# Last queries' steps of a decoder kernel: the sine part of the rotations moved to GpSimd, tree operations and product additions interleaved differently, and one block product issued earlier

## The chip, the cores and the metric

The kernel runs on one core of a Trainium2 chip. The engines of a core have instruction queues of their own: TensorE (PE; its weight loads are listed as PEld), VectorE (DVE), ScalarE (ACT), GpSimd (POOL) and SyncE (SP, which here only issues DMAs; ACT issues some too). The metric is the device time of one execution in microseconds (us), given as the median of several runs.

## The reference

Two decoder layers over x of shape (2, 512, 1024), all in float32 at the interfaces. The change touches only the start of the second layer's attention:

```python
x = x + _L0_xattn_ref(_layernorm(x), ctx, ...)      # quantized product
x = x + _L0_ffn_ref(_layernorm(x), ...)             # linear with routed low-rank part
x = x + _L1_xattn_ref(_layernorm(x), ctx, ctx, mask, wq, wk, wv, wo, 0)
x = x + _L1_ffn_ref(_layernorm(x), ...)             # linear with gated low-rank part

# in _L1_xattn_ref: 32 query heads, 8 key/value heads, 128 wide
q = _apply_rope(q, curr_seq_pos)                    # x * cos + rotate_half(x) * sin
raw = jnp.einsum('bhqd,bhkd->bhqk', q, k) / scale
attn = jax.nn.softmax(raw + mask, axis=-1)
out = jnp.einsum('bhqk,bhkd->bhqd', attn, v)
```

Queries are 512 long, keys and values 1024 long.

## The kernel before

**Products.** The large products are done as one level of a Strassen-like scheme: seven block products (`seven`, L270, in the order 1, 2, 6, 7, 5, 4, 3) give four blocks of 128 x 512. Each block product is four matmuls of 128x128 by 128x512 into a PSUM bank (`accumulate`, L345; its matmul is L347). The results are combined by additions on VectorE (L288, L291, L293, L297, L300). A finished block of queries is handed to `emit` (L664), which starts a rotation (`rope_steps`, L213). A rotation is two half copies on ScalarE (L216, L217: the rotated half of the block), then on VectorE `dst = acc * scale * cos` (L219), `rot = rot * sin` (L222) and `dst = dst + rot` (L223), and a DMA that writes the block to DRAM (L662).

**The last queries and the attention share steps.** Queries are made in eight groups of four heads. The eighth group (heads 28 to 31 of both batches, 2 x 7 = 14 block products, called a1, b1, a2, b2, then a6 a7 a5 a4 a3, then b6 b7 b5 b4 b3 after the two halves `head(0)` and `head(1)` and the block number) isn't made at once: `attention` (L836) draws its products one by one with `next(extra["products"])`. Of each rotation only the ScalarE copies are issued with the product; the rest is put on a list `later` and issued further on in the step.

**A step of the attention** is one turn of the loop at L860, with n from -2. It works on three heads at once: `new` = head n+2, `mid` = head n+1, `old` = head n.

- Scores of `new` (L743): four times two matmuls (L748) into a two-bank PSUM tile `wide`, each followed on VectorE by the addition of the mask into SBUF (L762). There are two `wide` tiles, taken in turn, so scores 2 needs the L762 of scores 0 to be done.
- The maximum over keys, `tree` (L766): four VectorE operations L770, L772, L774 (128 x 1024, all operands in SBUF) and L776 (128 x 512).
- Block products of the last queries or, for n over 4, of the output projection (`projection`, L824, through `seven_onto`, L304).
- `turn_sum` of `old` and `turn_maximum` of `new` (L779, L783): four transposes on TensorE into a `wide` tile (L712), a reduction on VectorE (L714, for the sum also L785), and a trip through DRAM by ScalarE's DMA queue (L721, L727) that comes back spread over all partitions. A `wide` tile used here is free for scores again once L714 is done.
- `exponential` of `mid`, twice: L794 on VectorE (128 x 2048, one operand in SBUF, the maximum in PSUM, put there by ScalarE at L790), L797 on ScalarE, and the sums over keys on GpSimd (L800; then L803, L804, L805).
- `attend` of `old`, twice four matmuls (L811), each time after one of the two turns; ScalarE copies the result out (L819), GpSimd multiplies by the reciprocal sum one step later (L822).

In the loop the order on TensorE, VectorE, ScalarE and GpSimd is the order of the program; each queue runs its instructions in that order. SyncE's queue holds the loads of queries, keys, values and weights, and the writes L662. At n = 4, 8, ... GpSimd also adds up operands of the projection (L245 to L253).

The number of products drawn in step n is in L1121:

```python
extra = {-2: 3, -1: 2, 0: 2, 1: 2, 2: 2, 3: 2, 4: 1}
```

and phase two and three of a step are, before the change (L892 to L927, shortened):

```python
for _ in range(3 + k % 2):
    next(stretches, None); next(tree, None)
...
for _ in range(extra.pop(n, 0)):
    next(extra["products"]); next(tree, None)
...
for steps in (tree, *extra["later"]):
    for _ in steps: pass
```

The functions in full, with the line numbers that the profile uses:

Of the kernel before, what the change touches and what calls it, by code (L numbers as in the profile page):

```python
# [15 lines left out]
ALU = mybir.AluOpType  # L16
# [6 lines left out]
GRP = NH // NKV  # L23
# [12 lines left out]
ATT_SCALE = float(np.float32(1.0) / np.sqrt(np.float32(DH)))  # L36
# [3 lines left out]
def decoder_kernel(  # L40
# [25 lines left out]
    nc = tc.nc  # L66
# [12 lines left out]
    def u8(shape, dtype=F32):  # L79
        return new(shape, "u8", 14, dtype)  # L80

    def u4(shape, dtype=F32):
        return new(shape, "u4", 17, dtype)

    def u2(shape, dtype=F32):
        return new(shape, "u2", 10, dtype)
# [61 lines left out]
    sin_t = [const.tile([P, HALF], F32, name="sin_t"), None]  # L148
# [58 lines left out]

    def rope(dst, acc, half, scale):

        for _ in rope_steps(dst, acc, half, scale):  # L210
            pass

    def rope_steps(dst, acc, half, scale):  # L213

        rot = u2([P, HALF])
        nc.scalar.activation(rot[0:64, :], acc[64:128, :], AF.Copy, scale=scale)  # L216
        nc.scalar.activation(rot[64:128, :], acc[0:64, :], AF.Copy, scale=scale)  # L217
        yield
        nc.vector.scalar_tensor_tensor(  # L219
            dst, acc, scale, cos_t[half], ALU.mult, ALU.mult  # L220
        )
        nc.vector.tensor_tensor(rot, rot, sin_t[half], ALU.mult)  # L222
        nc.vector.tensor_tensor(dst, dst, rot, ALU.add)  # L223

# [2 lines left out]
    def left_sums(eng, *args):  # L229

        return last_of(left_steps(eng, *args))
# [38 lines left out]
    def seven(product, emit):  # L270

        banks = {}
        for i in (1, 2, 6, 7, 5, 4, 3):
            first = {2: 1, 4: 7, 3: 5}.get(i, i)
            if i == first:
                banks[i] = ps_b()
            acc = banks[first]  # L280
            product(i, acc, i == first)
            if i == 1:
                u, c22, c21 = u2([P, HALF]), None, None
                nc.scalar.copy(u, acc)
            elif i == 2:
                emit(0, 0, acc)
            elif i == 6:
                nc.vector.tensor_tensor(u, u, acc, ALU.add)  # L288
            elif i == 7:
                c22 = u2([P, HALF])  # L290
                nc.vector.tensor_tensor(c22, u, acc, ALU.add)  # L291
            elif i == 5:
                nc.vector.tensor_tensor(c22, c22, acc, ALU.add)  # L293
                emit(1, 1, c22)
            elif i == 4:
                c21 = u2([P, HALF])
                nc.vector.tensor_tensor(c21, u, acc, ALU.add)  # L297
                emit(1, 0, c21)
            else:
                nc.vector.tensor_tensor(u, u, acc, ALU.add)  # L300
                emit(0, 1, u)
            yield
# [42 lines left out]
    def accumulate(acc, pairs, start):  # L345
        for k, (lhsT, rhs) in enumerate(pairs):
            nc.tensor.matmul(  # L347
                acc,
                lhsT,
                rhs,  # L350
                start=start and k == 0,
                stop=k == len(pairs) - 1,
                skip_group_check=True,
            )
# [19 lines left out]
    def halves():  # L374
        return [u8([P, 2, D]) for _ in range(2)]
# [273 lines left out]
    def queries(q, h_ops, w, later=None):  # L649

        def head(m):
            def product(i, acc, start):
                accumulate(
                    acc,
                    [(w[i - 1][:, c, ts(m, P)], h_ops[i - 1][:, c, :]) for c in range(4)],
                    start,
                )

            def finish(i, j, src):
                dst = u2([P, HALF]) if (i, j) == (0, 0) else src  # L660
                yield from rope_steps(dst, src, 0, ATT_SCALE)
                nc.sync.dma_start(q_d[j][4 * q + 2 * i + m], dst)  # L662

            def emit(i, j, src):  # L664
                steps = finish(i, j, src)
                next(steps)
                if later is None:
                    next(steps, None)
                else:
                    later.append(steps)  # L670

            return seven(product, emit)

        return head(0), head(1)
# [49 lines left out]
    def from_row(row):  # L724

        t = u2([P, S])
        nc.scalar.dma_start(t, row.partition_broadcast(P))  # L727
        return t
# [107 lines left out]
    def attention(extra):  # L836

        total = B * NH
        heads, outs, kv = {}, {}, {}
        stretches = iter(())

        def begin(n):
            if n >= total:
                return
            gg = n // GRP
            if gg not in kv:
                b, g = gg // NKV, gg % NKV  # L850
                kT = u4([P, S2])
                nc.sync.dma_start(kT, kT_d[b][g])
                v = u4([P, NKT, DH])
                nc.sync.dma_start(v, v_d[b][g // 2][:, :, ts(g % 2, DH)])
                kv[gg] = kT, v
                outs[gg] = u8([P, GRP, S])
            heads[n] = Head(n, kv[gg], outs[gg][:, n % GRP, :])

        begin(0)
        for n in range(-2, total + GRP + 1):  # L860
            new, mid, old = heads.get(n + 2), heads.get(n + 1), heads.get(n)
            begin(n + 3)
            if new:
                for j in range(4):
                    new.scores(j)
            yield

            if n - 1 in heads:
                heads.pop(n - 1).normalize()
            if n == GRP - 1 or n == NH:  # L870
                x[n // NH] = halves()
                for t, d in zip(x[n // NH], x_d[n // NH]):
                    nc.sync.dma_start(t, d)

            if GRP <= n <= total and n % GRP == 0:
                oT = outs.pop(n // GRP - 1)
                sums = u8([P, 3, 2, 256])
                places = iter(range(3))
                o_ops = left_sums(
                    nc.gpsimd,  # L880
                    oT[:, 0:2, 0:256],
                    oT[:, 2:4, 0:256],
                    oT[:, 0:2, 256:S],
                    oT[:, 2:4, 256:S],
                    lambda: sums[:, next(places)],
                )
                following = n // GRP - 1, o_ops
            tree = new.tree() if new else iter(())
            k = (n - 1) % GRP
            if n > GRP and k == 0:  # L890
                gg, o_ops = following
                stretches = projection(gg // NKV, o_ops, dict(w_ops))  # L892
            for _ in range(3 + k % 2):
                next(stretches, None)
                next(tree, None)
            if n > GRP and gg + 1 < B * NKV:
                for i in {2: (1, 6, 2), 3: (7, 5, 4, 3)}.get(k, ()):
                    w_ops[i] = output_operand((gg + 1) % NKV, i)
            for _ in range(extra.pop(n, 0)):
                next(extra["products"])  # L900
                next(tree, None)
            if n == GRP:
                w_ops = {i: output_operand(0, i) for i in (1, 6, 2, 7, 5, 4, 3)}
            for steps in (tree, *extra["later"]):
                for _ in steps:
                    pass
            extra["later"].clear()
            yield

            if mid:  # L910
                mid.place_maximum()
            if old:
                old.turn_sum()
                old.attend(0)
            if mid:
                mid.exponential(0)
            if old:
                old.den = from_row(old.den)
            if new:
                new.turn_maximum()  # L920
            if mid:
                mid.exponential(1)
            if new:
                new.nmx = from_row(new.nmx)
            if old:
                old.attend(1)
            yield  # L927
# [106 lines left out]
    for b in range(B):  # L1034
# [4 lines left out]
        for i, stage in enumerate((keys, keys, values, values)):  # L1039
# [7 lines left out]
            if i == 1 and b == 1:  # L1047
# [7 lines left out]
                hs, steps = normed(0, u8, 2)  # L1055
# [19 lines left out]
    for b in range(B):  # L1075
        main = linear(b, token_sums(hs, eights()), w_ops, lambda: tT[b], bl_t)
        if b == 0:
            hs, steps = normed(1, u8, 2)
# [24 lines left out]
    later = []  # L1103
# [14 lines left out]

    extra = {-2: 3, -1: 2, 0: 2, 1: 2, 2: 2, 3: 2, 4: 1}  # L1121
    steps = attention({**extra, "products": main, "later": later})
    stats = all_moments(0)
    last = {"zT": [None] * B, "w": [None] * 7, "h": [None] * 7}
# [42 lines left out]
    for i in range(2):  # L1167
        n = 44 + 4 * i
# [16 lines left out]
    with tc.manual_schedule(  # L1185
# [6 lines left out]
        for i in range(3 * (B * NH + 2)):  # L1192
            next(steps)
            n, phase = divmod(i, 3)
# [121 lines left out]
```

## Time and profile before

| | |
|---|---|
| median of 3 runs | 2494.17 us (2492.08 to 2495.93) |
| the profiled execution's own time | 2491.89 us |
| its span, first to last instruction | 2490.1 us |
| mean granted TensorE clock | 0.992 |
| VectorE busy | 1852.5 us (74%) |
| ScalarE busy | 527.9 us (21%) |
| GpSimd busy | 1011.8 us (41%) |
| the steps n = -2 to 4, and n = 5 up to the end of its projection products | about 937 to 1108 us of the span |
| rotations of the eighth group, VectorE part (L219, L222, L223) | first at 957.70, last at 1091.09 us |

Times in views of the trace are microseconds from the start of the span, and "us" columns are durations. A bracket like `[3.32 <-DVE small L714]` says how long the engine was idle before the instruction, and which instruction's end released it. "x8" counts instructions; each float32 matmul shows as two records, so a block product is 8 records, the scores of a head 16. In rows by stretch of time, each engine has its busy time and count, and PEclk is the TensorE clock that was granted, 1.00 being full speed.

### The profile page before, as it was taken

To read this page: it belongs to the slowest core of one execution; us is meant where nothing else is said; L and a number is where in the kernel's file an instruction comes from. 1 tells how busy PE (TensorE), PEld (TensorE's weight loads), DVE (VectorE), ACT (ScalarE), POOL (GpSimd) and SP (SyncE) were. 2 spreads that over 40 slices of the span, in tenths; PEclk is the share of its full clock that TensorE was granted. 3 is DMA by queue.
4 is the path that set the end of the run, shared out by engine and by line. 5 is a ranking of instruction groups with operands and counts; after the bars stand their busy time and mean duration, and the time that the engine had idled before them with its cause. 6 is when DMAs were issued, how large, how long until landed. Compare 5 with 4: busy or idle time off the path is not lost.

```text
span 2490.1 us, 19684 instructions
## 1 busy us (share of the span) xinstructions
PE 2434.2 (98%) x6848; PEld 1214.5 (49%) x6856; DVE 1852.5 (74%) x2036; ACT 527.9 (21%) x615; POOL 1011.8 (41%) x536
## 2 busy tenths in 40 slices
PE   7999999999999998989999999999999999999999
PEld 3477458654444443434444444444444444445454
DVE  5848774345886557988888888888898888887552
ACT  1201221011222222232222222222222222222100
POOL 0000010111000001557676767676777676667421
PEclk8999999999999999999999999999999999999999
DMA  7225233012895221343323322442334233323301
GB/s 264 103 92 204 75 124 106 26 68 106 283 329 199 76 93 47 102 131 107 84 80 109 109 83 80 138 150 79 114 106 130 62 104 114 104 74 110 127 26 43
DMA packets 148243, 283.83 MB, mean 114 GB/s; under 512 B 29296, under 2 KB 47232, under 8 KB 146352
## 3 DMA queue, kind: packets, MB, share of 16 engines
q1 hardware_dynamic: 107888, 242.25, 28.7%
q10 hardware_dynamic: 39824, 39.60, 6.6%
q8 instruction: 55, 0.90, 0.2%
q0 software_dynamic: 432, 0.71, 0.1%
q14 instruction: 44, 0.36, 0.0%
HBM read 221.44 MB, written 61.08 MB: 113 GB/s over the span
## 4 chain that ended last, share of the span: by engine, by line
PE 59%; DVE 7%; POOL 2%; issue 2%; DMA 1%; ACT 1%; SPq 0%; POOLq 0%; DVEq 0%; ACTq 0%
PE b L347 26%; PE wide L748 15%; PE b L811 15%; PE wide L712 2%; DVE u L794 2%; DMA u<-in_wo_dram 1%; PE wide L937 1%; DVE u L772 1%; DVE u L774 1%; DVE small L714 1%; POOL u L804 1%; POOL u L803 0%; DVE u L762 0%; DVE u L222 0%; DVE u L219 0%
## 5 line engine op out<-in xcount | busy, mean ns | idle before, releaser
L347 PE MATMUL b<-u,u 128*128 128x512 f32 (+1 forms) x3648 | 1408.6, 543 | 25.3 <-DVE u L291 10.8
L347 PEld LDWEIGHTS b<-u,u 128*128 128x128 f32 x3648 | 691.4, 191 | 707.5 <-issue 619.4
L748 PE MATMUL wide<-u,u 128*128 128x512 f32 x1024 | 456.9, 597 | 15.7 <-DVE small L714 8.5
L811 PE MATMUL b<-u,u 128*128 128x512 f32 x1024 | 461.2, 593 | 0.0
L800 POOL TENSOR_TENSOR u<-u 128x1024 f32<-128x1024 f32 x64 | 151.6, 2369 | 747.4 <-DMA row<-small 385.0
L762 DVE TENSOR_TENSOR u<-wide,u 128x1024 f32<-128x1024 f32 x256 | 312.7, 1224 | 128.2 <-PE wide L748 127.8
L797 ACT ACTIVATE u<-u 128x2048 f32<-128x2048 f32 x128 | 244.6, 1911 | 675.7 <-DVE u L794 626.4
L748 PEld LDWEIGHTS wide<-u,u 128*128 128x128 f32 x1024 | 193.4, 191 | 268.0 <-issue 176.8
L794 DVE TENSOR_TENSOR u<-u,b 128x2048 f32<-128x2048 f32 x128 | 290.0, 2266 | 0.0
L811 PEld LDWEIGHTS b<-u,u 128*128 128x128 f32 x1024 | 186.7, 192 | 185.2 <-issue 185.2
L322 POOL TENSOR_TENSOR u<-u,u 128x512 f32<-128x512 f32 x120 | 189.4, 1599 | 195.0 <-DVE u L320 175.4
L320 DVE TENSOR_TENSOR u<-u,b 128x512 f32<-128x512 f32 x200 | 135.7, 679 | 135.1 <-PE b L347 135.1
L803 POOL TENSOR_TENSOR u<-u,u 128x1024 f32<-128x1024 f32 x64 | 150.8, 2356 | 35.6 <-ACT u L797 34.6
L804 POOL TENSOR_TENSOR u<-u,u 128x1024 f32<-128x1024 f32 x64 | 151.9, 2374 | 5.0
L822 POOL TENSOR_TENSOR u<-u,u 128x512 f32<-128x512 f32 x64 | 119.9, 1873 | 21.4 <-DMA u<-row 21.4
L1053 POOL DMA_DIRECT2D u<-in_b_dram x1 | 0.6, 558 | 301.8 <-PE wide L450 301.8
L216 ACT ACTIVATE u<-u 64x512 f32<-64x512 f32 x72 | 45.2, 628 | 344.6 <-DVE u L293 167.3
L712 PEld LDWEIGHTS wide<-ident,u 128*128 128x128 f32 x512 | 80.2, 204 | 64.6 <-issue 54.7
L770 DVE TENSOR_TENSOR u<-u 128x1024 f32<-128x1024 f32 x64 | 111.4, 1741 | 0.0
L772 DVE TENSOR_TENSOR u<-u,u 128x1024 f32<-128x1024 f32 x64 | 106.3, 1660 | 0.2
L805 POOL TENSOR_TENSOR u<-u 128x512 f32<-128x512 f32 x64 | 102.0, 1594 | 5.0
L774 DVE TENSOR_TENSOR u<-u,u 128x1024 f32<-128x1024 f32 x64 | 97.4, 1522 | 0.2
(125 smaller groups left out, 1552.3 us busy)
## 6 DMA issues: line engine op xcount, KB each, us to landing
u<-row ACTq DMA_DIRECT2D x128, 256.0 KB, 3.7
u<-wo SPq DMA_DIRECT2D x64, 512.0 KB, 4.0
u<-in_wo_dram SPq DMA_DIRECT2D x48, 512.0 KB, 4.5
u<-in_wq_dram SPq DMA_DIRECT2D x32, 512.0 KB, 4.0
q<-u SPq DMA_DIRECT2D x64, 256.0 KB, 2.1
u<-in_wo_dram SPq DMA_DIRECT2D x16, 1024.0 KB, 8.1
wo<-u SPq DMA_DIRECT2D x32, 512.0 KB, 3.7
u<-q SPq DMA_DIRECT2D x64, 256.0 KB, 4.1
```

Of the source, the lines that this page charges most:

```text
L320: nc.vector.tensor_tensor(c, c, acc, ALU.add)
L322: nc.gpsimd.tensor_tensor(c, c, u, ALU.add)
L347: nc.tensor.matmul(acc, lhsT, rhs, start=start and k == 0, stop=k == len(pairs) - 1, skip_group_check=True,)
L748: nc.tensor.matmul(sc[:, ts(n, HALF)], self.kT[:, ts(2 * j + n, P)], self.qT, start=True, stop=True,)
L762: nc.vector.tensor_tensor(self.e[j // 2][:, js, :], sc.rearrange("p (k q) -> p k q", k=2), mask[j], ALU.add)
L772: nc.vector.tensor_tensor(m, m, e[1][:, 0:2, :], ALU.max)
L794: nc.vector.tensor_tensor(e, e, self.nmf.unsqueeze(1).to_broadcast([P, 4, S]), ALU.add)
L797: nc.scalar.activation(e, e, AF.Exp)
L800: nc.gpsimd.tensor_tensor(d, e[:, 0:2, :], e[:, 2:4, :], ALU.add)
L803: nc.gpsimd.tensor_tensor(d, d, e[:, 0:2, :], ALU.add)
L804: nc.gpsimd.tensor_tensor(d, d, e[:, 2:4, :], ALU.add)
L811: nc.tensor.matmul(self.acc, self.v[:, k, :], self.e[j][:, k % 4, :], start=(k == 0), stop=(k == NKT - 1),)
```

## The change

The rotation takes its engine as an argument. For the eighth group of queries L222 and L223 (the multiplication by the sine and the last addition) are issued on GpSimd; L219 and the ScalarE copies stay, and all other rotations stay as they were. In steps with n of 4 and less, the operations of the maximum's tree are no longer issued ahead of the loop over products: before each product two of them are issued, and what is left after the last product. The pending rotations are issued by `rotate()`, after `turn_sum` of the old head (or, where there is no old head yet, after `turn_maximum` of the new one, which thereby comes ahead of the exponentials in steps -2 and -1) instead of right behind the tree. In the table of products, step -1 draws three instead of two and step 3 one instead of two: the order of the products stays, and the sixth, eighth, tenth and twelfth are each issued one step sooner.

```diff
-    def rope_steps(dst, acc, half, scale):
+    def rope_steps(dst, acc, half, scale, eng):
...
-        nc.vector.tensor_tensor(rot, rot, sin_t[half], ALU.mult)
-        nc.vector.tensor_tensor(dst, dst, rot, ALU.add)
+        eng.tensor_tensor(rot, rot, sin_t[half], ALU.mult)
+        eng.tensor_tensor(dst, dst, rot, ALU.add)
...
-                yield from rope_steps(dst, src, 0, ATT_SCALE)
+                eng = nc.vector if later is None else nc.gpsimd
+                yield from rope_steps(dst, src, 0, ATT_SCALE, eng)
                 nc.sync.dma_start(q_d[j][4 * q + 2 * i + m], dst)
...
+        def rotate():
+            for rotation in extra["later"]:
+                next(rotation, None)
+            extra["later"].clear()
...
-            for _ in range(3 + k % 2):
+            for _ in range(3 + k % 2 if n > GRP else 0):
                 next(stretches, None)
                 next(tree, None)
...
             for _ in range(extra.pop(n, 0)):
+                for _ in range(2):
+                    next(tree, None)
                 next(extra["products"])
-                next(tree, None)
...
-            for steps in (tree, *extra["later"]):
-                for _ in steps:
-                    pass
-            extra["later"].clear()
+            for _ in tree:
+                pass
             yield
 
             if mid:
                 mid.place_maximum()
             if old:
                 old.turn_sum()
+            elif new:
+                new.turn_maximum()
+            rotate()
+            if old:
                 old.attend(0)
             if mid:
                 mid.exponential(0)
             if old:
                 old.den = from_row(old.den)
-            if new:
-                new.turn_maximum()
+                if new:
+                    new.turn_maximum()
             if mid:
                 mid.exponential(1)
...
-    extra = {-2: 3, -1: 2, 0: 2, 1: 2, 2: 2, 3: 2, 4: 1}
+    extra = {-2: 3, -1: 3, 0: 2, 1: 2, 2: 2, 3: 1, 4: 1}
```

More of the change, by code (lines that the diff above doesn't have):

```diff
@@ L208, in rope @@
     def rope(dst, acc, half, scale):
-        for _ in rope_steps(dst, acc, half, scale):
+        for _ in rope_steps(dst, acc, half, scale, nc.vector):
             pass
-    def rope_steps(dst, acc, half, scale):
+    def rope_steps(dst, acc, half, scale, eng):
         rot = u2([P, HALF])
```

## The prediction

> **What bounds the kernel now.** I read the page first, then stretches of time around the steps that change, then what TensorE waited for there, then the timelines of TensorE, VectorE and GpSimd. The page:
>
> ```profile
> PE 2434.2 (98%) x6848; PEld 1214.5 (49%) x6856; DVE 1852.5 (74%) x2036; ACT 527.9 (21%) x615; POOL 1011.8 (41%) x536
> ```
>
> TensorE sets the end; only its lost time can be won. From 1107.4 us on, the listing of TensorE shows no more gaps in the following steps, so a gain before that should last to the end. Three of the nine stretches of the early steps (busy time and count of each engine, then granted clock):
>
> ```profile
> core 0: us, PE busy (x) PEld busy (x) DVE busy (x) ACT busy (x) POOL busy (x), PEclk, DMA share, GB/s
> ...
> 972.49:993.14 20.65, 17.33 (x38) 7.47 (x37) 17.72 (x16) 3.82 (x2) 8.34 (x4) 0.83 0.12 38
> ...
> 1039.04:1060.59 21.55, 21.55 (x58) 10.06 (x57) 18.78 (x17) 4.30 (x3) 10.56 (x5) 1.00 0.33 91
> ...
> 1081.56:1107.43 25.87, 20.99 (x52) 9.10 (x53) 22.45 (x19) 7.32 (x8) 18.78 (x10) 1.00 0.46 137
> ```
>
> The turns of step 2 and the scores and products of step 3 (middle row) are pure TensorE. The turns of step 4 and the scores and products of step 5 (last row) lose some 5 us with VectorE 87% busy, and the scores of step 0 (first row) lose 3.3 us and run at a granted clock of 0.83. What TensorE waited for between 935 and 1100 us (total, times, longest):
>
> ```profile
> PE wide L748 <- DVE small L714: 8.5, 5, 3.3
> ...
> PE wide L748 <- DVE u L762: 5.7, 4, 1.6
> ...
> PE wide L712 <- POOL u L805: 1.1, 1, 1.1
> ...
> PE wide L712 <- DVE u L776: 0.9, 1, 0.9
> ```
>
> So scores wait for a `wide` tile, because VectorE comes late to L714 and L762. The largest case, first on TensorE, then on VectorE:
>
> ```profile
> 972.49 0.63 PE L712 MATMUL wide<-ident,u 128*128 128x128 f32 x4
> 972.96 1.88 PE L748 MATMUL wide<-u,u 128*128 128x512 f32 x4
> 978.16 8.28 PE L748 MATMUL wide<-u,u 128*128 128x512 f32 x12 [3.32 <-DVE small L714]
> ```
>
> ```profile
> 972.69 0.69 DVE L288 TENSOR_TENSOR u<-u,b 128x512 f32<-128x512 f32 x1 [1.26 <-PE b L347]
> 973.30 0.68 DVE L219 SCALAR_TENSOR_TENSOR u<-b,cos_t 128x512 f32<-128x512 f32 x1
> 973.90 0.68 DVE L222 TENSOR_TENSOR u<-u,sin_t 128x512 f32<-128x512 f32 x1
> 974.61 0.69 DVE L223 TENSOR_TENSOR u<-u,u 128x512 f32<-128x512 f32 x1
> 975.22 2.28 DVE L794 TENSOR_TENSOR u<-u,b 128x2048 f32<-128x2048 f32 x1
> 977.42 0.68 DVE L714 TENSOR_REDUCE small<-wide 128x4 f32<-128x512 f32 x1
> 978.02 2.27 DVE L794 TENSOR_TENSOR u<-u,b 128x2048 f32<-128x2048 f32 x1
> 980.22 1.22 DVE L762 TENSOR_TENSOR u<-wide,u 128x1024 f32<-128x1024 f32 x1
> ```
>
> The transposes are done at 973, but L714 runs behind a rotation and an L794; and the 12 records after it take 8.28 us where 12 others take 5.42.
>
> **The sum before.** From its listing, undisturbed TensorE work costs: block product 3.44, a head's scores 6.87 (1.72 a pair), four transposes 0.47, half an attend 3.44. From 937.07 to the end of step 5's products (1107.59) there are 8 heads of scores, 14 products, three projection products of 1.72, 12 turns, 5 attends: 148.3 us in 170.5, so 22.2 are lost: 2.1 in the scores of step -2 (ahead of every edit), 2.0 in those of step -1, 6.6 in step 0, 2.5 in step 2, 1.6 in step 4, 2.5 at its two turns, 4.8 in step 5's scores. A gap costs some 0.25 us beyond its length (8 records take 3.70 behind one, 3.43 otherwise).
>
> **The change, step by step.** VectorE's pitches: short operation 0.61, L794 2.2, L762 1.15 to 1.22, tree operation 1.24 alone and 2.17 beside GpSimd.
>
> *Step -2.* L714 no longer sits behind the rotation of a2, which waited for ScalarE until 957.70: it starts at 956.9, ends at 957.6, before the second pair of scores (958.6) needs its tile. **2.0 us gone.** The L762 of pair 0 comes after L219 at 958.7, early enough for pair 2 at 960.3.
>
> *Step -1 with its third product.* Product a7 has to run anyway. Behind its end, VectorE has L291 0.65, L714 0.61, L219 0.61, two L794 4.4, L762 1.2, in all 7.5 us; TensorE covers transposes and two pairs, 0.47 + 3.43 = 3.9. L714 now comes in time (1.3 us behind the product), but **pair 2 then waits for the L762 behind both L794: 3.6 us,** against 3.3 before. The wait changes its name, no more.
>
> Does the clock drop again? The row: after a 3.3 us gap the clock is 0.50 from 977.2 to 983.9. The Trainium skill (TensorE: Matmul & The Clock Gate, Part 1) says the clock halves after an idle window of some 3.4 us, and that windows run freely. Taken as written, a gap of 3.6 holds a whole idle window only by luck ((3.6 - 3.4)/3.4, 6%), and no clock time would be lost. The trace contradicts: 3.3 was enough here, and a 2.3 us gap ending at 349.3 us also led to a granted 0.51. I follow the row: 5.8 us at half clock, **2.9 lost.** Step 0's scores lose 3.6 + 0.25 + 2.9 = 6.75 after, 6.6 before.
>
> *Steps 0 to 2.* Two rotations in step 0 (a5, a4), one in 1 (a3), one in 2 (b5); before: one, two, none. Each takes 0.61 of VectorE instead of 1.9. L714 of the sum follows the last product addition directly; both L714 are over 1.8 to 3.3 us before their tiles are needed, and VectorE is free 1.2 to 1.9 us before the L762 of pair 0 can start. In step 2 b5 is the last product, so L219 waits 0.7 us for ScalarE's two copies; the 1.2 hold that. **2.5 us gone.**
>
> *Tree order.* Two of four tree operations now stand ahead of the first addition, where three or four stood; with two products L776 is 0.61 later. Its reader, the turn of the maximum, comes 3.9 us behind the last product: hidden at nothing. In step 3, with one product (18.1 us of TensorE instead of 21.6), that cover is gone: tree beside GpSimd 4.2 + 0.6 + 2.5 us behind L762 ends 0.4 after attend's first half, **0.65 with the restart.**
>
> *Steps 4 and 5.* The rotation of b3 now takes 0.7 (before, 0.93 + 1.75 + 0.69 beside GpSimd's operand sums). The turn of the sum waits for L805, 0.75; the turn of the maximum for L776 behind a tree slowed throughout, 1.6; pair 2 of step 5 for L762, 0.4. With restarts 3.5, against 8.9. **5.4 gone.**
>
> *GpSimd.* 16 operations of 128x512 are new. Nearest rows:
>
> ```profile
> 1079.38 2.12 POOL L805 TENSOR_TENSOR u<-u 128x512 f32<-128x512 f32 x1
> ...
> 1087.57 1.27 POOL L250 TENSOR_TENSOR u<-u 128x512 f32<-128x512 f32 x1
> ```
>
> 1.27 alone, 2.1 to 2.25 beside the tree. They follow L219 and run beside L794, L714, L762, not beside the tree: I take 1.27, 2.6 a rotation. They stand ahead of L800, before which GpSimd idles 6 to 14 us: hidden, except in step 0 (two rotations delay L800 by 2, with 3 to spare at the next turn) and step 4, where b3's pair is queued behind L822 and four operand sums. There L805 of head 5 ends 1.0 before its turn: nothing at 1.27, 1 us at 2.25.
>
> What speaks against the move is the skill's SBUF page (SBUF — State Buffer, Who interferes with whom): a VectorE instruction with two SBUF inputs and a GpSimd instruction that reads SBUF take one port pair, for the whole instruction. The trace shows it for the tree (1.2 against 2.17) and not for instructions with one PSUM input: 128 L794 lie between 2254 and 2280 ns, and L762 keeps 1.22 during L803. A lock on everything would cost 16 x 1.27 = 20 us of VectorE, some 13 on the path; by the rows, nothing. Below nothing: GpSimd can't make VectorE faster than the 1.3 us a rotation already counted.
>
> *DMAs.* The writes L662 wait up to 3 us longer at SyncE, ahead of loads of queries, keys and values used 10 us or more later: nothing. Longer-held SBUF tiles: at most 10 alive in step 1, of 10; nothing, upper end 2 us.
>
> **Sum:** after, 2.1 + 6.75 + 0.65 + 3.5 = 13.0 lost instead of 22.2; 9.2 gone. Own time 2491.89 - 9.2 = 2482.7; the median lies 2.3 above the profiled execution, so **2485.0 us.**
>
> **Rivals.**
> - *The clock doesn't drop* (the page's rule as written): 2.9 more, 12.1 gone, 2482.1. For: windows run freely. Against: both rows above. Chance 0.17.
> - *Steps 3 to 5 give it back:* two steps of one product are VectorE's, its tree always beside a GpSimd that is later now; if the 5.4 of steps 4 and 5 come back as waits for L776 and L805, 3.8 is left: 2490.4. For: L805 has 1 us to spare. Against: 2.4 us of slow VectorE work are removed right there. Chance 0.20.
> - *GpSimd's rotations hold VectorE* ahead of L794, h us each. With the slack above, 7h - 4.9 falls on the path (b2, two in step 0, a3, b5, b4, b3), equal to the gain at h = 2.0. At two operations between 1.27 and 2.25, middle 3.5, it is 19.6: 2504.6. For: the page's rule. Against: L794's narrow spread. Chance 0.07.
> - *It doesn't do what it says:* TensorE's order of scores and turns is unchanged, and only the 2.0 of step -2 come: 2492.2. Chance 0.05.
>
> **Numbers.** The forecast has 0.51. A measurement of this kernel can tell some 0.2% (5 us) from no change. Faster by more: 0.51 + 0.17 and half of the second rival, which straddles the limit, 0.78; within: the other half and the last rival, 0.15; slower: 0.07. The range reaches from the clock rival less its 2 us of scatter, 2480.0, to the giving back, 2490.6.
>
> **What would show it.** Right: no wait of the second pair of step -1 for L714; at the start of step 0 a wait for L762 of 3 to 4 us and a clock of 0.5 behind it; no gaps in steps 1 and 2; L794 still 2.27; small waits for L776 and L805 in steps 3 and 4; step 6 about 9 us earlier, then no difference. Wrong: L794 over 2.4, or gaps for L805 in step 5, or lost time beyond step 6.

## The result, and the profile after

The changed kernel takes 2481.54 us (median of 6 runs, 2477.93 to 2484.01) against 2493.43 us (6 runs, 2490.43 to 2495.93): ratio 0.995, 95% interval 0.9939 to 0.996. A second set of runs (e9) gave 2481.79 against 2493.73, ratio 0.9954 (0.9942 to 0.9967). So 11.9 us are gone in both; 9.2 were forecast. Line numbers behind the rotation shift by one: L712, L714, L748, L762, L770 to L776, L794, L805 are now L713, L715, L749, L763, L771 to L777, L795, L806.

The page's busy times:

```profile
PE 2436.6 (98%) x6848; PEld 1216.4 (49%) x6856; DVE 1839.0 (74%) x2020; ACT 527.7 (21%) x615; POOL 1029.8 (41%) x552
```

VectorE has 16 instructions less and 13.5 us less work, GpSimd 16 and 18.0 more; TensorE's busy time is nearly as it was (2434.2 before). What TensorE waited for between 935 and 1112 us (total, times, longest):

```profile
PE wide L749 <- DVE u L763: 5.1, 2, 3.6
PE wide L713 <- DVE u L777: 0.9, 1, 0.9
PE wide L713 <- POOL u L806: 0.8, 1, 0.8
```

The 8.5 us of waits for the reduction, L714 before, are gone altogether. One wait of 3.6 for L763 is new. TensorE's timeline, cut to what matters:

```profile
956.29 7.03 PE L749 MATMUL wide<-u,u 128*128 128x512 f32 x16
...
973.46 0.63 PE L713 MATMUL wide<-ident,u 128*128 128x128 f32 x4
973.92 3.60 PE L749 MATMUL wide<-u,u 128*128 128x512 f32 x8
981.13 6.56 PE L749 MATMUL wide<-u,u 128*128 128x512 f32 x8 [3.60 <-DVE u L763]
...
1059.53 0.72 PE L713 MATMUL wide<-ident,u 128*128 128x128 f32 x4
...
1063.52 7.43 PE L749 MATMUL wide<-u,u 128*128 128x512 f32 x16
...
1075.20 0.75 PE L713 MATMUL wide<-ident,u 128*128 128x128 f32 x4 [0.81 <-POOL u L806]
...
1080.26 0.72 PE L713 MATMUL wide<-ident,u 128*128 128x128 f32 x4 [0.88 <-DVE u L777]
```

The scores of step -1 run through (7.03 for 16 records is the undisturbed figure), those of step 0 stop for 3.60 us before the third pair, and the 8 records behind the gap take 6.56 us, where 3.70 is usual behind a gap. VectorE in front of that gap:

```profile
973.66 0.69 DVE L291 TENSOR_TENSOR u<-u,b 128x512 f32<-128x512 f32 x1 [2.75 <-PE b L347]
974.26 0.69 DVE L715 TENSOR_REDUCE small<-wide 128x4 f32<-128x512 f32 x1
974.86 0.68 DVE L219 SCALAR_TENSOR_TENSOR u<-b,cos_t 128x512 f32<-128x512 f32 x1
975.46 4.48 DVE L795 TENSOR_TENSOR u<-u,b 128x2048 f32<-128x2048 f32 x2
979.85 2.35 DVE L763 TENSOR_TENSOR u<-wide,u 128x1024 f32<-128x1024 f32 x2
```

L715 is now early, and the wait moved to the L763 behind both L795, which VectorE could only begin after product a7.

**Two measures.** Call "early length" the time from the first scores of step -2 to the start of the turn behind step 5's projection products, so that a wait of that turn counts: 170.4 us before, 159.9 after (158.8 in e9's profile). The 10.5 us saved are not all in this execution's own time (2491.89 before, 2484.01 after, 7.9 less), because TensorE waited longer far behind the early steps. Its timeline there, before and then after:

```profile
1941.44 0.75 PE L712 MATMUL wide<-ident,u 128*128 128x128 f32 x4 [1.71 <-POOL u L805]
```

```profile
1932.07 0.97 PE L713 MATMUL wide<-ident,u 128*128 128x128 f32 x4 [2.62 <-POOL u L806]
1932.83 5.09 PE L812 MATMUL b<-u,u 128*128 128x512 f32 x8
```

The code there is unchanged; eight records took 5.09 where 3.60 is usual, at a granted clock of about 0.5. Over the 14 profiles of this study, the time from the end of the early length to the first gating matmul of the last linear stage varies from 1185.1 to 1189.2 us without a difference in its instructions, and the start of step -2 from 936.0 to 941.3. So one profile's own time tells little under 3 us, and the experiments are read by early length first and by the median of their runs second.

### The profile page after: what moved, and what is told of

The parts are those of the page before. It is cut to its first block, busy times and chain, and to the rows that moved or that the text cites. A ratio compares the mean times of both kernels' runs of the same rounds, so it can differ in the third digit from the quotient of the medians.

```text
span 2482.2 us, 19693 instructions
## 1 busy us (share of the span) xinstructions
PE 2436.6 (98%) x6848; PEld 1216.4 (49%) x6856; DVE 1839.0 (74%) x2020; ACT 527.7 (21%) x615; POOL 1029.8 (41%) x552
## 4 chain that ended last, share of the span: by engine, by line
PE 73%; DVE 7%; POOL 2%; issue 2%; DMA 1%; ACT 1%; POOLq 0%; SPq 0%; ACTq 0%; DVEq 0%
PE b L347 38%; PE wide L749 16%; PE b L812 15%; PE wide L713 2%; DVE u L795 1%; PE wide L204 1%; DMA u<-in_wo_dram 1%; PE wide L946 1%; PE b L636 1%; DVE u L763 1%; POOL u L805 1%; DVE u L775 1%; DVE u L773 0%; POOL u L804 0%; DVE u L320 0%
## 5 line engine op out<-in xcount | busy, mean ns | idle before, releaser
L749 PE MATMUL wide<-u,u 128*128 128x512 f32 x1024 | 455.5, 596 | 7.1 <-DVE u L763 6.2
L763 DVE TENSOR_TENSOR u<-wide,u 128x1024 f32<-128x1024 f32 x256 | 313.0, 1225 | 135.7 <-PE wide L749 134.3
L798 ACT ACTIVATE u<-u 128x2048 f32<-128x2048 f32 x128 | 244.6, 1911 | 654.3 <-DVE u L795 572.3
L749 PEld LDWEIGHTS wide<-u,u 128*128 128x128 f32 x1024 | 194.1, 191 | 257.0 <-issue 178.2
L795 DVE TENSOR_TENSOR u<-u,b 128x2048 f32<-128x2048 f32 x128 | 290.2, 2269 | 0.0
L222 POOL TENSOR_TENSOR u<-u,sin_t 128x512 f32<-128x512 f32 x8 | 11.7, 1457 | 387.2 <-ACT u L217 387.2
L805 POOL TENSOR_TENSOR u<-u,u 128x1024 f32<-128x1024 f32 x64 | 151.6, 2369 | 5.0
L713 PEld LDWEIGHTS wide<-ident,u 128*128 128x128 f32 x512 | 80.1, 204 | 65.8 <-issue 54.6
L771 DVE TENSOR_TENSOR u<-u 128x1024 f32<-128x1024 f32 x64 | 110.9, 1732 | 0.0
L773 DVE TENSOR_TENSOR u<-u,u 128x1024 f32<-128x1024 f32 x64 | 105.2, 1644 | 0.2
L806 POOL TENSOR_TENSOR u<-u 128x512 f32<-128x512 f32 x64 | 100.5, 1570 | 5.0
```

Of the source, the lines that this page charges most:

```text
L713: nc.tensor.transpose(tr[:, t, :], src[:, t, :], ident)
L749: nc.tensor.matmul(sc[:, ts(n, HALF)], self.kT[:, ts(2 * j + n, P)], self.qT, start=True, stop=True,)
L763: nc.vector.tensor_tensor(self.e[j // 2][:, js, :], sc.rearrange("p (k q) -> p k q", k=2), mask[j], ALU.add)
L795: nc.vector.tensor_tensor(e, e, self.nmf.unsqueeze(1).to_broadcast([P, 4, S]), ALU.add)
L798: nc.scalar.activation(e, e, AF.Exp)
L805: nc.gpsimd.tensor_tensor(d, d, e[:, 2:4, :], ALU.add)
```

## The experiments

Where the third pair of step 0 is late, the time lost to the halved TensorE clock differs from execution to execution, so the table gives it apart. It is what the records behind the gap of step 0 took beyond 3.70 us (for the kernel before, 12 records beyond 5.42). e1 and e10 lose another 1.8 and 1.9 us in this way behind a gap of step 5.

| kernel | median us | ratio (interval) | early length | of it half clock in step 0 |
|---|---|---|---|---|
| before | 2493.4 to 2494.7 | 1 | 170.4 | 2.9 |
| changed | 2481.54 | 0.995 (0.9939, 0.996) | 159.9 | 2.9 |
| e9 changed, again | 2481.79 | 0.9954 (0.9942, 0.9967) | 158.8 | 1.7 |
| e1 sine on VectorE | 2492.34 | 0.9995 (0.9987, 1.0002) | 167.3 | 1.6 |
| e10 the same again | 2491.57 | 0.9991 (0.9983, 1.0) | 167.6 | 1.7 |
| e2 sine on GpSimd alone | 2484.15 | 0.9961 (0.9949, 0.9973) | 160.0 | 0 |
| e3 old order of turns | 2484.85 | 0.9967 (0.9955, 0.9979) | 160.3 | 0 |
| e4 old table | 2479.89 | 0.9943 (0.993, 0.9956) | 157.5 | 1.7 |
| e8 old tree | 2485.87 | 0.9968 (0.9956, 0.9981) | 160.5 | 1.5 |
| e7 GpSimd's part doubled | 2489.3 | 0.9978 (0.9966, 0.999) | 163.0 | 0 |
| e6 filler in the gap | 2480.53 | 0.9947 (0.9934, 0.9959) | 157.3 | 0 |
| e5 early exponentials | 2480.35 | 0.9943 (0.993, 0.9957) | 154.1 | 0 |
| e11 the same again | 2476.99 | 0.9933 (0.992, 0.9945) | 154.2 | 0 |
| e12 and another table | 2477.87 | 0.9937 (0.9925, 0.995) | 155.1 | 0 |

Less the half-clock time, the changed kernel has 157.0 and 157.1 in its two profiles: the early steps repeat within 0.1 us.

**e1 and e10: everything but GpSimd.**

```diff
-                eng = nc.vector if later is None else nc.gpsimd
+                eng = nc.vector
```

> The changed kernel with L222 and L223 of the eighth group back on VectorE; order, tree and table stay as changed. Theory (VectorE's 1.3 us a rotation ends on TensorE only where VectorE had no slack: 1.3 at b2, 0.9 in step 0, 1.3 at b4, 2.0 at b3): 5.5 us over the changed kernel, about 2487, with the gap at the start of step 0 at 4.9 instead of 3.6 us. Rival (the order does all the work, the engine is of no account): 2481.5. Rival (GpSimd's rotations hold VectorE, so that taking them away helps): below 2480.

Measured: 2492.34, ratio 0.9995, which can't be told from the kernel before. The repeat was made beside the changed kernel:

> The changed kernel with L222 and L223 of the eighth group on VectorE, now beside the changed kernel. Theory (its early steps are 7.5 us longer than the changed kernel's in the first profiles): 7 to 9 us over the changed kernel of this call. Rival (the first time, 10.8 us over, was right, and more than the early steps is lost): 10 to 12.

2491.57, 9.8 over the changed kernel run beside it (e9), between theory and rival. The rival of e1 that makes the engine of no account is out, and so is the one that GpSimd's rotations hold VectorE. But the theory's 5.5 us was too small. TensorE's waits of e1 in the early steps:

```profile
PE wide L749 <- DVE u L763: 8.4, 5, 4.9
PE wide L749 <- DVE small L715: 1.9, 1, 1.9
PE wide L713 <- POOL u L806: 1.7, 2, 0.9
PE wide L713 <- DVE u L777: 0.9, 1, 0.9
```

The gap of step 0 is 4.9, as worked out; but there are waits in steps that I had taken to be covered (0.6 in step -1, a second wait for L806 in step 3), and in step 4 the rotation on VectorE costs more than 2:

```profile
1085.48 0.95 DVE L219 SCALAR_TENSOR_TENSOR u<-u,cos_t 128x512 f32<-128x512 f32 x1
1086.36 1.75 DVE L222 TENSOR_TENSOR u<-u,sin_t 128x512 f32<-128x512 f32 x1
1088.14 1.64 DVE L223 TENSOR_TENSOR u<-u,u 128x512 f32<-128x512 f32 x1
```

GpSimd at the same time, with the projection's operand sums:

```profile
1085.85 1.71 POOL L250 TENSOR_TENSOR u<-u 128x512 f32<-128x512 f32 x1
1087.52 1.71 POOL L253 TENSOR_TENSOR u<-u,u 128x512 f32<-128x512 f32 x1
```

L222 and L223 take 1.75 and 1.64 instead of 0.68, and L795 of head 5 starts 3.3 us later for these two. The ends show that the engines take turns here: L250 ends at 1087.56, L222 0.55 behind it, L253 1.12 behind L222, L223 0.55 behind L253. The later L795 makes L715 late, TensorE waits 1.86 for it in step 5, and the 12 records behind that gap take 7.21 us instead of 5.42, at half clock. So e1 lost 1.8 us of clock that the theory didn't have; without the half clock of both places its early length is 7.0 over the changed kernel's.

**e2: GpSimd alone.** The kernel before, with only this:

```diff
-        nc.vector.tensor_tensor(rot, rot, sin_t[half], ALU.mult)
-        nc.vector.tensor_tensor(dst, dst, rot, ALU.add)
+        eng.tensor_tensor(rot, rot, sin_t[half], ALU.mult)
+        eng.tensor_tensor(dst, dst, rot, ALU.add)
...
+                eng = nc.vector if later is None else nc.gpsimd
```

> The kernel before with only L222 and L223 of the eighth group on GpSimd; order of the turns, tree and table as before. Theory (what counts is when VectorE reaches L714 and L762, and every way of taking 1.3 us a rotation out of its queue helps): most of the gain comes with this part alone, 2482 to 2485; the wait for L714 in step -1 falls from 1.8 to 0.6 us, the 3.3 us gap of step 0 becomes two gaps of about 1.9 and 1.7, and steps 2, 4 and 5 lose 3 us instead of 9. Rival (the gain comes from the order of the turns): under 3 us of gain, 2491.

Measured 2484.15, 10.0 under the kernel before that ran beside it. The theory holds in size, and in place for steps -1 and 0; its early waits are

```profile
PE wide L749 <- DVE u L763: 4.6, 4, 1.4
PE wide L749 <- DVE small L715: 2.9, 3, 1.9
```

with 0.48 in step -1, and 1.88 and 1.34 in step 0, behind which the clock stayed up: 2.9 of the 10.4 us by which the early length fell are the half clock that the kernel before lost there. Steps 2 to 5 still lose 5.4 us (11.4 before), more than the 3 of the theory. So **moving the sine part carries most of the gain**, and the three edits of the order, which gain about 2 us without it (e1, e10: 1.9 and 2.2, at the edge of what their intervals can tell), bring about as much on top of it (11.9 against 10.0).

**e3: old place of the rotations and of the turn of the maximum.** 

```diff
             for _ in tree:
                 pass
+            rotate()
             yield
...
-            elif new:
-                new.turn_maximum()
-            rotate()
-            if old:
                 old.attend(0)
...
             if old:
                 old.den = from_row(old.den)
-                if new:
-                    new.turn_maximum()
+            if new:
+                new.turn_maximum()
```

> The changed kernel with the rotations back right behind the tree, and the turn of the maximum back between the exponentials in steps -2 and -1; GpSimd, tree and table stay. Theory: 0.8 us are lost in step -1 (L714 behind L219 again), and step 0's gap of 3.6 becomes two, about 2.5 and 1.5; if the clock then doesn't drop, 2.9 come back: 2479 to 2483. Rival (the order of the turns is what removed the waits): 2488 or more.

2484.85, inside neither range. The forecast gaps of step 0 came (1.99 and 1.34, clock up), but in step 4 L219 stands ahead of L715 and beside GpSimd's sums takes 1.76 us, and TensorE waits 0.87 for L777 in step 3 and 0.92 for L763 in step 5. The early length is 3.3 over the changed kernel's without half clock. I had worked out only steps -2 to 0.

**e4: old table of products.**

```diff
-    extra = {-2: 3, -1: 3, 0: 2, 1: 2, 2: 2, 3: 1, 4: 1}
+    extra = {-2: 3, -1: 2, 0: 2, 1: 2, 2: 2, 3: 2, 4: 1}
```

> The changed kernel with the old table of products (two in step -1, two in step 3). Theory: the sooner product fills no gap, because the gap at the start of step 0 is VectorE's chain behind the last product of step -1 whichever that is; 0 to 1 us over the changed kernel, 2481.5 to 2482.5, and step 0 still has its 3.6 us gap. Rival (the sooner product fills time that TensorE lost): 3.4 us more, 2485.

2479.89, 1.7 under the changed kernel where 0 to 1 over it was forecast, with a gap of 3.49 in step 0. The sooner product wins nothing: without half clock the early length is 155.8 against 157.0. With two products in step 3 again, the waits of step 4's scores (0.4) and for L806 (0.81) are gone, and that for L777 is 1.35 instead of 0.88. With both intervals some 0.0025 wide, the time itself doesn't settle which table is better.

**e8: old place of the tree.** 

```diff
-            for _ in range(3 + k % 2 if n > GRP else 0):
+            for _ in range(3 + k % 2):
                 next(stretches, None)
                 next(tree, None)
...
             for _ in range(extra.pop(n, 0)):
-                for _ in range(2):
-                    next(tree, None)
                 next(extra["products"])
+                next(tree, None)
```

> The changed kernel with the old place of the tree's operations in steps up to 4 (three or four ahead of the first product's addition). Theory: no turn waits for the difference: within 1 us of the changed kernel, 2481 to 2482.5. Rival (tree ahead of additions is what keeps the turns of the maximum from waiting): 2 to 4 us more.

2485.87, 4 us over: the theory fails. The size is the rival's, but most of the waits are not those of the turn of the maximum. VectorE in step 4 of this kernel:

```profile
1078.45 1.64 DVE L777 TENSOR_TENSOR u<-u 128x512 f32<-128x512 f32 x1
1080.01 0.67 DVE L300 TENSOR_TENSOR u<-u,b 128x512 f32<-128x512 f32 x1
1080.61 0.68 DVE L715 TENSOR_REDUCE small<-wide 128x4 f32<-128x512 f32 x1
...
1082.08 0.92 DVE L219 SCALAR_TENSOR_TENSOR u<-u,cos_t 128x512 f32<-128x512 f32 x1 [0.58 <-ACT u L217]
```

The addition L300 stands behind the whole tree, so ScalarE's copies start late, L219 waits for them, and L795 and the next L763 come later: TensorE waits 1.34 for that L763 in step 5 (0.4 in the changed kernel), and in step 3 0.26 for L806 and 0.40 for L777. The early length shows 2.0 of it without half clock; where the other 2 us of the time lie, one profile doesn't say.

**e7: GpSimd's part of the rotations doubled.**

```diff
         eng.tensor_tensor(dst, dst, rot, ALU.add)
+        if eng is nc.gpsimd:
+            eng.tensor_tensor(dst, dst, rot, ALU.subtract)
+            eng.tensor_tensor(dst, dst, rot, ALU.add)
```

> The changed kernel with two more GpSimd operations in each rotation (dst - rot, then dst + rot), so 16 more of 128x512. Theory (GpSimd holds VectorE only beside instructions with two SBUF operands, and idles ahead of L801 except in step 4): L795 stays at 2.27 us, L806 of head 5 comes 2.6 us later and TensorE waits about 2 us for it in step 5: 2482 to 2484.5. Rival (GpSimd's operations hold all of VectorE): 2.5 us a rotation on the path, about 13 to 18 us, 2495 or more.

2489.3, 7.8 over the changed kernel's first median: too much for the theory, too little for the rival. The same instruction as L795 (here L798) keeps 2254 to 2280 ns, so GpSimd's operations don't hold it. What is late is GpSimd's own chain, here its end at step 5:

```profile
1091.08 1.28 POOL L226 TENSOR_TENSOR u<-u,u 128x512 f32<-128x512 f32 x1
...
1097.18 3.21 POOL L808 TENSOR_TENSOR u<-u,u 128x1024 f32<-128x1024 f32 x1
1100.46 2.13 POOL L809 TENSOR_TENSOR u<-u 128x512 f32<-128x512 f32 x1
```

There are no gaps from the rotation to L809 (L806 of the changed kernel), and TensorE waits 5.4 us for L809 in three places: 2.9 in step 5, 1.6 in step 1, and the 0.8 of step 4 that the changed kernel has too. Moved later, the chain also runs beside the tree: L808 takes 3.21 instead of 2.36.

**e6: work in the gap.**

```diff
+            if j == 2 and self.b == 0 and self.hd == 2:
+                spare = ps_b()
+                for n in range(4):
+                    nc.tensor.matmul(spare, self.kT[:, ts(n, P)], self.qT, start=True, stop=True)
             sc = ps_wide()
```

> The changed kernel with four extra matmuls (128x128 by 128x512, their result read by nobody) between the second and third pair of scores of head 2, that is in the gap at the start of step 0. Theory: they take 3.4 us of a 3.6 us gap, delay nothing, and keep the clock up: 2.5 to 3 us under the changed kernel, about 2478.7, granted clock 1.00 there. Rival (what runs slow there isn't the clock, or the gap has nothing to do with it): no gain, 2481.5 or up to 3.4 us more.

The stretches around the former gap (busy time and count by engine, then granted clock):

```profile
976.50:980.00 3.50, 3.50 (x9) 1.33 (x7) 3.50 (x3) 2.81 (x2) 1.10 (x1) 1.00 0.47 150
980.20:984.00 3.80, 3.74 (x9) 1.82 (x10) 2.36 (x3) 0.82 (x1) 3.64 (x3) 1.00 0.28 66
```

Against the changed kernel's

```profile
981.10:987.60 6.50, 6.47 (x9) 2.79 (x10) 2.33 (x2) 0.78 (x1) 6.26 (x4) 0.55 0.11 39
```

the clock stays at 1.00 and the early length is 157.3, the changed kernel's less its half-clock time and 0.3 more: four useless matmuls delay next to nothing. The median, 2480.53, is 1 us lower, which its interval can't tell from nothing. One profile alone would not show that the filler kept the clock up, because in e7 it stayed up behind the same 3.60 us gap; the section on the prediction shows what tells these cases apart. The forecast of 2.5 to 3 us in the time isn't shown, since the changed kernel doesn't always pay it in full.

**e5 and e11: exponentials ahead of the waiting additions.**

```diff
-            for _ in range(extra.pop(n, 0)):
+            for i in range(extra.pop(n, 0)):
                 for _ in range(2):
                     next(tree, None)
+                if n == -1 and i == 1:
+                    mid.place_maximum()
+                    mid.exponential(0)
+                if n == -1 and i == 2:
+                    mid.exponential(1)
                 next(extra["products"])
...
-            if mid:
+            if mid and n != -1:
                 mid.place_maximum()
...
-            if mid:
+            if mid and n != -1:
                 mid.exponential(0)
...
-            if mid:
+            if mid and n != -1:
                 mid.exponential(1)
```

> The changed kernel, but in step -1 the maximum of head 0 is placed and its L795 of the first half issued ahead of the second product, that of the second half ahead of the third product, so that VectorE does them while it waits for these products. Theory: the 3.6 us gap at the start of step 0 goes, and with it the half clock behind it (2.9 us) and the restart: 6 to 7 us under the changed kernel, about 2475. Rival (the gap only moves behind another VectorE instruction): 0 to 2 us, 2480 to 2481.5. Rival (the clock drops without the gap): 3.6 us, 2478.

2480.35, by its time in the range of the rival that only moves the gap; the repeat, beside the changed kernel:

> The kernel with both exponentials of head 0 ahead of the products' additions in step -1, now beside the changed kernel. Theory (its early steps are 5.8 us shorter, and nothing takes that back later): 4 to 7 us under the changed kernel of this call. Rival (the gain is given back behind the early steps): 0 to 2 us.

2476.99, 4.8 under the changed kernel run beside it (e9), as the theory had it. VectorE in step -1 of e5:

```profile
971.25 0.69 DVE L777 TENSOR_TENSOR u<-u 128x512 f32<-128x512 f32 x1
971.86 2.28 DVE L795 TENSOR_TENSOR u<-u,b 128x2048 f32<-128x2048 f32 x1
974.06 0.68 DVE L288 TENSOR_TENSOR u<-u,b 128x512 f32<-128x512 f32 x1
974.66 2.28 DVE L795 TENSOR_TENSOR u<-u,b 128x2048 f32<-128x2048 f32 x1
976.86 0.68 DVE L291 TENSOR_TENSOR u<-u,b 128x512 f32<-128x512 f32 x1
977.45 0.68 DVE L715 TENSOR_REDUCE small<-wide 128x4 f32<-128x512 f32 x1
```

No idle time is left ahead of L288 and L291, and step 0 has no gap. The early length falls by 2.9 besides the half clock, not by 3.85 (gap and restart): step 3 now waits 0.94 for L777, because two of its tree operations run beside GpSimd (L771 2.29, L773 2.17) where in the changed kernel one does. This version is ahead of both kernels: 0.9943 and 0.9933 of the kernel before.

**e12: e5 with another table.**

```diff
-    extra = {-2: 3, -1: 3, 0: 2, 1: 2, 2: 2, 3: 1, 4: 1}
+    extra = {-2: 3, -1: 3, 0: 2, 1: 2, 2: 1, 3: 1, 4: 2}
```

> As the one before, with the products of step 2 one and of step 4 two (table -2: 3, -1: 3, 0: 2, 1: 2, 2: 1, 3: 1, 4: 2). Theory: a step with one product is short of cover for VectorE by about 0.9 us, and by 2.5 where GpSimd's operand sums slow the tree (step 4); moving the single product from step 4 to step 2 wins 1 to 2 us in the early steps, which a time can hardly tell: 2473 to 2479. Rival (cover is not what step 4 lacks): the waits for L806 and L777 stay in step 4, no gain.

2477.87, early length 155.1 against 154.2: no gain. The waits leave step 4 and reappear in steps 2 and 3 (0.93 and 0.87 for L777, 0.32 for L806) and at L763 of step 5 (1.35). A step with one product is short of cover wherever it stands.

**e9: the changed kernel again, without an edit.**

> The changed kernel itself, beside the next three: how far the times of one kernel differ from call to call. Theory: 2481.5 within 2 us, and waits of the early steps as in its first profile; what differs between its executions lies outside these steps.

2481.79, with the early waits of the first profile (3.60, 0.81, 0.88); only the half-clock time differs.

## Why the prediction was right, point by point

- *Step -2, 2.0 us:* right. No wait in step -1's scores.
- *Step 0's wait changes its name:* right, 3.60 behind two L795 for 3.6. That the sooner product doesn't matter for it is shown by e4 (3.49 with the old table).
- *Half clock, 2.9 us:* right in the profile that was taken (6.56 instead of 3.70), **too much as a mean.** The same 3.60 gap cost 2.9, 1.7 (e9), 1.5 (e8) and nothing (e7: 3.70 for the 8 records) in four executions. In the clock's record of each execution the changes lie on a grid of 3.41 us, and the grid lies differently against the program each time. Stretches of this grid around the gap, in the changed kernel, in e9 and in e7 (length, busy time and count of each engine with TensorE first, then the granted clock):

```profile
976.68:980.10 3.42, 0.84 (x2) 0.01 (x1) 3.42 (x3) 2.04 (x2) 0.70 (x2) 1.00 0.48 153
980.10:983.51 3.41, 2.38 (x3) 1.18 (x4) 2.10 (x2) 1.78 (x1) 3.33 (x2) 0.50 0.23 77
983.51:986.92 3.41, 3.41 (x5) 1.35 (x4) 1.23 (x1) 0.00 (x0) 3.33 (x2) 0.50 0.00 0
...
978.73:982.15 3.42, 1.13 (x3) 0.65 (x4) 3.37 (x3) 2.76 (x2) 2.42 (x2) 1.00 0.33 117
982.15:985.56 3.41, 3.41 (x5) 1.35 (x5) 1.23 (x1) 0.00 (x0) 3.33 (x2) 0.50 0.06 22
...
978.80:982.21 3.41, 1.45 (x4) 0.38 (x2) 3.41 (x2) 2.26 (x2) 3.25 (x3) 1.00 0.00 0
982.21:985.63 3.42, 1.78 (x4) 0.87 (x5) 2.72 (x3) 2.11 (x2) 3.33 (x3) 1.00 0.56 170
```

  Behind a stretch with 0.84 or 1.13 us of busy TensorE the clock is halved, for one stretch if that one is busy throughout (e9), for two if it isn't (2.38, the changed kernel). In e7 the gap is shared between two stretches, 1.45 and 1.78 are busy, and the clock stays up. So the loss depends on where the grid lies, which I could not know: that the profile before the change and the one behind it both lost 2.9 is luck. In e6 the only gap left there is 0.17 us, so that no stretch is low wherever the grid lies. The border between enough and too little isn't sharp: in step 5 of e1 the clock was halved behind a stretch with 1.55. The Trainium skill (TensorE: Matmul & The Clock Gate, Part 1) has windows that run freely, as this grid does. My estimate from its window, a chance of 6%, took a window to be idle throughout; here a quarter to a third of it was busy.
- *Steps 0 to 2, no gaps:* right.
- *Tree order, nothing, and 0.65 lost in step 3:* the wait in step 3 was 0.1 (L713 at 1059.53 starts without a listed gap), since only one of its tree operations ran beside GpSimd. The terms of that line, added up, don't give its 0.4 either: the last L762 ends 1.3 behind the scores, 7.3 more make 8.6, and product, transposes and half an attend are 7.35, so 1.3. "Hidden at nothing" was wrong: e8 shows 2 us in the early steps and 4 in the time. I priced L777 and left out who waits for the addition: ScalarE's copies, then L219.
- *Steps 4 and 5, 3.5 lost:* 3.0 measured from the start of step 4's scores. L806 0.81 for 0.75, L763 0.4 for 0.4 in step 5 and another 0.4 in step 4, which I didn't have, L777 0.88 for 1.6: the tree was slowed to 1.69 and 1.64 at its end, not to 2.17.
- *GpSimd at 1.27:* 1.27 to 1.79 measured, mean 1.46 for L222. It starts as soon as ScalarE's copies are done, ahead of L219, which I had put first, and so sometimes beside the tree, whose L777 takes 1.64 instead of 0.69 beside the first of these:

```profile
968.06 1.29 POOL L222 TENSOR_TENSOR u<-u,sin_t 128x512 f32<-128x512 f32 x1 [8.09 <-ACT u L217]
...
1084.12 1.28 POOL L222 TENSOR_TENSOR u<-u,sin_t 128x512 f32<-128x512 f32 x1
...
1094.02 2.14 POOL L806 TENSOR_TENSOR u<-u 128x512 f32<-128x512 f32 x1
```

  L806 of head 5 ended at 1096.2, 0.5 ahead of its turn: half of the 1 us to spare was used, and e7 shows what follows when all is.
- *The lock rival:* against. L795 stayed at 2255 to 2282 ns, and e1, without these operations on GpSimd, is slower, not faster.
- *Lost time beyond step 6*, a sign of being wrong, is there in the first profile: the 2.62 gap at 1932 and the half clock behind it. e9's profile of the same kernel has no half clock there and the kernel before waits 1.71 at that place, so it isn't shown to come from the change.
- *The sum:* 9.2 forecast, 11.9 measured. The early length of the profile fell by 10.5: step 3 (0.5) and steps 4 and 5 (0.5) were too dear, and 0.3 less was lost in step -2's scores, ahead of every edit, which is chance. The remaining 1.4 between 10.5 and 11.9 is of the size of the mean half-clock loss that I overstated, which is argued from the spread of the table, not shown by itself. The median, 2481.54, is nearer to the clock rival's 2482.1 than to the forecast's 2485.0, so the time alone doesn't decide between them; the profile, at half clock behind the gap, does for its own execution.

## What to carry to other kernels

In an in-order queue, ask of every instruction that waits what independent work stands behind it: here two exponentials of 2.2 us stood behind an addition that waited for TensorE, and moving them ahead (e5) closed a gap that the change had only renamed. Work taken from an engine is worth its full time only where that engine had no slack, so price it step by step. Measure the parts of a change apart: here the sine part alone has 10.0 of the 11.9 us (e2), and of the three edits of the order the table gains nothing (e4). For an operation that is moved, follow its readers one engine further than the one that you are looking at.

## What the runs showed of the hardware

A gap of 3.60 us on TensorE was followed by 0 to 2.9 us of half-clock loss in different executions, a gap of 2.62 by 1.5, one of 1.86 by 1.8 and 1.9 (step 5 of e1 and e10), and the pairs 1.88 and 1.34 (e2) and 1.99 and 1.34 (e3) by none. Not the length alone counts, but how busy TensorE is in each stretch of the 3.41 us grid.

VectorE and GpSimd take turns where VectorE reads both operands from SBUF. Of the 192 tree operations of 128x1024 in the changed kernel's trace, 145 take over 1.3 us, and each of these ends 1.08 us (1.080 to 1.088) after a GpSimd instruction has ended; alone such an operation takes 1.22. So the tree's 1.22 became 2.17, L219's 0.69 became 1.76 (e3), and GpSimd's 2.36 became 3.21 (e7): a duration in these rows includes the wait for the other engine. With one operand in PSUM nothing of this is seen in the 128 L795, which stay at 2255 to 2282 ns.
